# The seam between two graph layers of one fused kernel: moving the first queries and keys of layer 1 into the last turn of layer 0, and the last output products into sequence

## The chip, the core and the metric

The kernel runs on one core of a Trainium2 chip. The metric is device time in microseconds (us), the median of three runs. A core has five engines with a queue of instructions each: PE (TensorE, matrix products), DVE (VectorE), ACT (ScalarE), POOL (GpSimd) and SP (SyncE, which here issues every DMA). They run side by side and wait for each other through semaphores; within an engine, order is that of the program.

## The reference, cut to what matters

128 graphs of 64 nodes, 768 features. Layer 0 is a graph attention of 12 heads with a gate, layer 1 a masked attention of 6 heads; each ends in a layer norm over a residual.

```python
# layer 0
h    = einsum('bnd,ade->bane', x, W);  th = tanh(h)
attn = leaky(th @ w_src + swap(th @ w_dst))          # masked by adj, softmax
fo   = elu(attn @ h + b)
gate = sigmoid(x @ H_w.T + H_b)
x1   = layernorm(x + gate * fo + (1 - gate) * x)
# layer 1
q, k, v = x1 @ Wq + bq, x1 @ Wk + bk, x1 @ Wv + bv   # 6 heads of 128
p    = softmax(q @ k.T / sqrt(128) + mask(adj))
out  = layernorm(x1 + (p @ v) @ Wf + bf)
```

## The kernel before, in words

Everything is float32. The 8192 rows are 64 tiles of 128 rows (two graphs each), taken as 32 pairs. Every large product (768 x 768 weight) is done by a seven-product block scheme: class `Job` (line 150) multiplies 7 combinations of input blocks with 7 combinations of weight blocks, each a group of three accumulating matmuls into a PSUM bank, and `way_out` (line 182) adds the results into the output on ACT and DVE. `step` (line 208) issues one product on PE and then the way out of the product before it. The weight combinations are four subtractions per weight (`weight_sums`, line 129: T1 to T4; the loaded blocks are B11, B21, B22 and, until it is overwritten, T3), the input combinations four more (`block_sums`, line 135). A job's product number picks its weight block: 1 B11, 2 B21, 3 B22, 4 T4, 5 T1, 6 T2, 7 T3. In names of tiles a product's bank starts with y, z or x.

**Layer 0** (lines 236 to 626). Turn p of a loop makes h and gate of pair p and, half a turn behind, finishes pair q = p - 1: it normalises attention, makes x1, and computes the value rows v of layer 1 from it. The 21 products of a turn are in a hand-written order, `TURN` (line 52); a letter is the job (h, g, v; u is v of the turn before, whose last two products come then), a digit the product. The other steps are hung on positions of that order by `at(pos, ...)` (lines 584 to 614): for a tile t, `probs_by_nodes` transposes its probabilities (pTp), `attend` multiplies them with h (av), `features` divides (rden, fo), `elu1`, `gated`, `stats` and `normed` make x1, `by_features` transposes it (x1Tp). A pair's second tile goes first: 63 before 62 in pair 31. The tiles pTp, av and x1Tp share two PSUM banks with the tag "m". Each turn writes x1, its transpose x1T and v to DRAM. The loop runs over 34 turns: turn 32 has no new pair, so only u4, u3 and the seven v products remain for PE, and turn 33 has the last two v products.

**Layer 1** (lines 629 to 877). 16 groups of four tiles. Its storage is a new pool, `sb1`, opened when `sb0` of layer 0 is closed; then bf, the three bias columns (`load_cols`, line 116), wq, the group's four blocks of x1T (a), adj, wk and wf are loaded in that order, and the weight sums are on DVE (lines 653 to 659); wq takes the storage of w0, wk that of hw, wf that of wv. For each group and each of three feature blocks fc, `woven` (line 831) runs a query job and a key job in the order `WOVEN` (line 46), one step of the generators beside it per product: `attention` of the block before (scores sp, softmax, transposes sT, context cp), `finish` (norms of the group before), or `residuals` (line 770: the x1 rows, plus bf on POOL, and the input sums of the output job on DVE). After a group's features come the output products of the group before. At the end (line 865 on, g = 16) the last attention and residuals are drained first, then the 14 output products of the last two pairs are woven, and their four norms follow.

PE, DVE, ACT and POOL follow the order of these calls; so does SP for its DMAs, and a DMA that has to wait (for its data or for the storage it writes) holds those behind it.

Of the kernel before, what the change touches and what calls it, by code (L numbers as in the profile page):

```python
# [9 lines left out]
F32 = mybir.dt.float32  # L10
# [40 lines left out]

TURN = [
# [6 lines left out]
def kernel(  # L59
# [61 lines left out]
    def load_weight(src, tag, name):  # L121

        w = wpool.tile([P, 7, HK, HALF], F32, tag=tag, name=name)
        view = src.rearrange("(kh kc p) (nh f) -> kh nh p kc f", p=P, kc=HK, nh=2)
        for block, kh, nh in ((B11, 0, 0), (B21, 1, 0), (B22, 1, 1), (T3, 0, 1)):
            nc.sync.dma_start(out=w[:, block], in_=view[kh, nh])
        return w

    def weight_sums(eng, w):
        eng.tensor_tensor(w[:, T1], w[:, T3], w[:, B11], ALU.subtract)  # L130
        eng.tensor_tensor(w[:, T2], w[:, B22], w[:, T1], ALU.subtract)  # L131
        eng.tensor_tensor(w[:, T4], w[:, B21], w[:, T2], ALU.subtract)
        eng.tensor_tensor(w[:, T3], w[:, B22], w[:, T3], ALU.subtract)

    def block_sums(eng, pool, tag, a11, a12, a21, a22, name):

        shape = [P, HK, a11.shape[-1]]
        s1, s2, s3, s4 = (
            pool.tile(shape, F32, tag=f"{tag}{i}", name=f"{tag}{i}_{name}", bufs=1)
            for i in range(1, 5)  # L140
        )
        steps = [
            lambda: eng.tensor_tensor(s1, a21, a22, ALU.add),  # L143
            lambda: eng.tensor_tensor(s2, s1, a11, ALU.subtract),
            lambda: eng.tensor_tensor(s3, a11, a21, ALU.subtract),
            lambda: eng.tensor_tensor(s4, a12, s2, ALU.subtract),
        ]
        return {1: a11, 2: a12, 3: s4, 4: a22, 5: s1, 6: s2, 7: s3}, steps
# [64 lines left out]
    def layernorm(dst, z, eps, name):  # L213
        stats = small.tile([P, 2, 6], F32, tag="stats", name=f"st_{name}")
        for half in range(2):
            V.bn_stats(stats[:, half, :], z[:, half * HALF : (half + 1) * HALF])  # L216
# [19 lines left out]
    with ExitStack() as ph:  # L236
        sb = ph.enter_context(tc.tile_pool(name="sb0", bufs=2))

        def load_rows(src, n, name):
            t = sb.tile([P, n], F32, name=name, bufs=1)  # L240
            nc.sync.dma_start(out=t, in_=src.partition_broadcast(P))
            return t

        def load_xT(p):
            t = sb.tile([P, KC, PAIR * P], F32, tag="xT", name=f"xT_{p}")
            nc.sync.dma_start(out=t, in_=xT[p])
            return t
# [9 lines left out]
        def sums_of(eng, tag, t, name):  # L257
            return block_sums(
                eng, sb, tag, t[:, :HK, :P], t[:, HK:, :P], t[:, :HK, P:], t[:, HK:, P:], name
            )  # L260

        xTs = {0: load_xT(0)}
        w0_w = load_weight(w0, "wa", "w0")
        hw_w = load_weight(hwT, "wb", "hw")
        wsd = sb.tile([P, 2, D], F32, name="wsd", bufs=1)
        nc.sync.dma_start(out=wsd[:, 0, :], in_=wdst.partition_broadcast(P))
        nc.sync.dma_start(out=wsd[:, 1, :], in_=wsrc.partition_broadcast(P))
        hb_bc = load_rows(hb, D, "hb_bc")
        b01_bc = load_rows(b0, E0, "b01_bc")
        A = {}  # L270
        A[0], x_steps = sums_of(G, "sx", xTs[0], "x0")
        for s in x_steps:
            s()
        weight_sums(V, w0_w)
        weight_sums(G, hw_w)
        V.tensor_scalar(b01_bc, b01_bc, 1.0, None, ALU.add)
        wv_w = load_weight(wv, "wc", "wv")
        weight_sums(V, wv_w)
# [75 lines left out]
        def products(t):  # L354

            h = st[t]["h"]
            th = sb.tile([P, 2, D], F32, tag="th", name=f"th_{t}")
# [195 lines left out]
        def value_sums(q):  # L553
            B[q], v_sums[q] = sums_of(V, "sv", x1Ts[q], f"v{q}")

        def x_sums(p):
            A[p], steps = sums_of(G, "sx", xTs[p], f"x{p}")
            for s in steps:
                s()

        v_sums = {}
        jobs = {}
        for p in range(NP + 2):
# [5 lines left out]

            plan = {}  # L570

            def at(pos, ok, *acts):
                if ok:
                    plan.setdefault(pos, []).extend(acts)
# [40 lines left out]

            for pos, (job, i) in enumerate(TURN):
                ok = {"h": new, "g": new, "v": old, "u": 0 <= p - 2 < NP}[job]
                if ok:
                    step(jobs["u" if job == "u" else job], int(i))
# [6 lines left out]
        flush()  # L626


    with ExitStack() as ph:
        sb = ph.enter_context(tc.tile_pool(name="sb1", bufs=2))  # L630
        W2 = PAIR * P

        bf_bc = sb.tile([P, D], F32, name="bf_bc", bufs=1)
        nc.sync.dma_start(out=bf_bc, in_=bf.partition_broadcast(P))
        bq_c, bk_c, bv_c = load_cols(bq, "bq_c"), load_cols(bk, "bk_c"), load_cols(bv, "bv_c")

        def load_group(g):

            blocks = []
            for m in range(2):  # L640
                for kh in range(2):
                    t = sb.tile([P, HK, W2], F32, tag=f"a{m}{kh}", name=f"a{m}{kh}_{g}", bufs=1)
                    nc.sync.dma_start(out=t, in_=x1T_d[2 * g + m][:, kh * HK : (kh + 1) * HK, :])
                    blocks.append(t)
            ad = load_adj(sb, GT * g, GT, f"adjg_{g}")
            bias = sb.tile([P, GT, N], F32, tag="bias", name=f"bias_{g}", bufs=2)
            V.tensor_scalar(bias, ad, 1.0, NEG1 / SCALE, ALU.subtract, ALU.mult)
            ops, steps = block_sums(G, sb, "sq", *blocks, f"q{g}")
            for s in steps:
                s()  # L650
            return ops, bias

        wq_w = load_weight(wq, "wa", "wq")
        weight_sums(V, wq_w)
        loaded = load_group(0)
        wk_w = load_weight(wk, "wb", "wk")
        weight_sums(V, wk_w)
        wf_w = load_weight(wf, "wc", "wf")
        weight_sums(V, wf_w)

        def feature_job(name, ops, w, fc, dst, b):


            def at(m, n):
                return dst[:, n, m * W2 : (m + 1) * W2]

            def bias(n):
                return b[:, n * HK + fc : n * HK + fc + 1]

            return Job(  # L670
                name,
                W2,
                lambda i, kc: (w[:, OF_B[i], kc, fc * P : (fc + 1) * P], ops[i][:, kc, :]),
                lambda mn, bk_: S.activation(at(*mn), bk_, AF.Identity, bias=bias(mn[1])),  # L674
                lambda mn, bk_: V.tensor_tensor(at(*mn), bk_, at(*mn), ALU.add),  # L675
                lambda bk_: S.activation(at(1, 0), bk_, AF.Identity, bias=bias(0)),
            )

        ctxT = {}

        def attention(g, fc, qT, kT, bias):


            v = sb.tile([P, GT, 2, E1], F32, tag="v1", name=f"v1_{g}_{fc}")
            for a in range(2):
                c0 = (a * J1 + fc) * E1
                for i in range(GT):
                    nc.sync.dma_start(
                        out=v[a * N : (a + 1) * N, i, :, :],
                        in_=v_d[GT * g + i][:, c0 : c0 + E1].rearrange("(g m) e -> m g e", m=N),  # L690
                    )
            yield
            yield
            yield
            sp = bank("m", f"sp_{g}_{fc}")
            for i in range(GT):
                for a in range(2):
                    for gr in range(2):
                        at = slice(i * P + gr * N, i * P + (gr + 1) * N)
                        T.matmul(  # L700
                            sp[gr * N : (gr + 1) * N, (i * 2 + a) * N : (i * 2 + a + 1) * N],
                            qT[:, a, at],
                            kT[:, a, at],
                            start=True,
                            stop=True,
                        )
            yield
            sc = sb.tile([P, GT, 2, N], F32, tag="sc", name=f"sc_{g}_{fc}")
            V.tensor_tensor(
                sc,  # L710
                sp.rearrange("p (i a m) -> p i a m", i=GT, a=2),
                bias.unsqueeze(2).to_broadcast([P, GT, 2, N]),
                ALU.add,
            )
            sc3 = sc.rearrange("p i a m -> p (i a) m")
            mx = small.tile([P, 2 * GT], F32, tag="mx1", name=f"mx1_{g}_{fc}")
            V.tensor_reduce(mx, sc3, AX.X, ALU.max)
            yield
            V.tensor_tensor(sc3, sc3, mx.unsqueeze(2).to_broadcast([P, 2 * GT, N]), ALU.subtract)
            S.activation(sc, sc, AF.Exp, scale=SCALE)  # L720
            yield
            yield
            den = small.tile([P, 2 * GT], F32, tag="den1", name=f"den1_{g}_{fc}")
            V.tensor_reduce(den, sc3, AX.X, ALU.add)
# [195 lines left out]
```

## Time and profile before

| | us |
|---|---|
| median of 3 runs (3020.79 to 3021.99) | 3021.93 |
| the profiled execution, device time | 3022.04 |
| its span, first to last instruction | 3020.0 |
| PE busy | 2931.3 (97%) |
| DVE busy | 1830.8 (61%) |
| ACT busy | 1006.5 (33%) |
| POOL busy | 805.5 (27%) |
| mean granted clock of PE | 0.986 of full |

The page gives one profiled execution: busy times of each engine, the span in 40 slices (75.5 us each; a digit is the busy share in tenths, PEclk the granted clock in tenths), queues of DMA, waits and groups of instructions. A line of the timeline has start and length in us, engine, line of the code, operation, output<-inputs, shape and count; brackets hold the idle time ahead of it on its engine and who ended it. A matmul group of three in the code shows as x6. The window view has, for a stretch, its length, busy time and count of PE, PEld, DVE, ACT and POOL, then the clock, the DMA share and GB/s. Layer 0 runs to about 1515 us of the span, layer 1 from about 1519 us.

### The profile page before, as it was taken

What the parts mean: (1) busy time and instruction counts of PE and PEld (TensorE: products, weight loads), DVE (VectorE), ACT (ScalarE), POOL (GpSimd) and SP (SyncE); (2) the same over time, 40 slices, a digit from 0 to 9 for tenths busy, and PEclk for the clock granted to TensorE, in tenths of its full rate; (3) what the DMA queues carried; (4) which work ended last, traced back from release to release, by engine and by line L of the source; (5) the groups of instructions that cost most, each with busy time, mean ns of one, the idle gap of its engine ahead of it and who ended that gap; (6) DMA issues with size and microseconds to landing.
All of it is one profiled execution on the core that took longest, in us unless ns stands there. A gap on an engine that the chain in (4) does not pass through costs nothing. (4 is left out here: it accounts for less than half of the span.)

```text
span 3020.0 us, 45321 instructions
## 1 busy us (share of the span) xinstructions
PE 2931.3 (97%) x18048; PEld 2029.7 (67%) x18048; DVE 1830.8 (61%) x3017; ACT 1006.5 (33%) x1761; POOL 805.5 (27%) x650
## 2 busy tenths in 40 slices
PE   6999999999999999999869999999999999999997
PEld 3666666666666666666558777787777787777784
DVE  5888888888888888888633344434344434344434
ACT  2444344344444444444412222222222222222221
POOL 4324324324323333333212111211211211211211
PEclk8999999999999999999879999999999999999998
DMA  4333333333333333333242111222111222111211
GB/s 168 115 112 109 116 118 107 112 120 112 108 121 114 109 117 119 107 113 114 90 146 86 62 57 58 85 85 79 62 57 57 85 85 79 62 57 57 85 64 63
DMA packets 174929, 284.81 MB, mean 94 GB/s; under 512 B 46208, under 2 KB 112768, under 8 KB 174720
## 3 DMA queue, kind: packets, MB, share of 16 engines
q1 hardware_dynamic: 174720, 281.92, 28.7%
q8 instruction: 143, 2.34, 0.3%
q14 instruction: 66, 0.54, 0.1%
HBM read 167.81 MB, written 101.06 MB: 89 GB/s over the span
## 5 line engine op out<-in xcount | busy, mean ns | idle before, releaser
L487 POOL TENSOR_TENSOR x<-gate,x 128x768 f32<-128x768 f32 x64 | 116.5, 1821 | 330.9 <-ACT gate L538 330.9
L780 POOL TENSOR_TENSOR y<-y,bf_bc 128x768 f32<-128x768 f32 x64 | 114.3, 1816 | 301.7 <-DMA y<-x1d 301.7
L804 DVE TENSOR_TENSOR y<-y_o,y 128x384 f32<-128x384 f32 x128 | 69.8, 553 | 178.0 <-PE y_o L173 171.0
L222 POOL TENSOR_TENSOR rs_b<-ve_b,minus_half 128x1 f32<-128x1 f32 x64 | 35.1, 549 | 483.6 <-DVE ve_b L220 480.7
L675 DVE TENSOR_TENSOR kT<-z_k,kT 128x256 f32<-128x256 f32 x96 | 40.5, 422 | 203.6 <-ACT kT L674 108.9
L173 PE MATMUL y_q<-a,wq 128*128 128x256 f32 x576 | 141.7, 382 | 17.4 <-DMA a<-x1Td 17.4
L360 POOL TENSOR_TENSOR th<-th,wsd 128x768 f32<-128x768 f32 x64 | 116.0, 1812 | 157.5 <-DVE th L359 157.5
L143 POOL TENSOR_TENSOR sq_q<-a,a 128x768 f32<-128x768 f32 x16 | 29.5, 1844 | 466.6 <-PE y_o L173 311.0
L674 ACT ACTIVATE qT<-y_q,bq_c 128x256 f32<-128x256 f32 x144 | 67.3, 468 | 244.6 <-PE y_q L173 222.8
L173 PE MATMUL y_k<-a,wk 128*128 128x256 f32 x576 | 144.9, 388 | 1.8 <-DMA wk<-in_wk_dram 1.8
L173 PE MATMUL y_g<-hw,sx_x 128*128 128x384 f32 x384 | 136.0, 491 | 10.5 <-DVE gate L336 10.5
L173 PE MATMUL z_k<-sq_q,wk 128*128 128x256 f32 x576 | 141.5, 382 | 4.1 <-DVE qT L675 4.1
L173 PE MATMUL y_o<-wf,so_o 128*128 128x384 f32 x384 | 134.4, 494 | 8.8 <-DVE y L804 8.8
L173 PE MATMUL y_h<-w,xT 128*128 128x384 f32 x384 | 136.3, 492 | 6.8 <-DMA w<-in_w_dram 6.8
L173 PE MATMUL y_k<-sq_q,wk 128*128 128x256 f32 x576 | 141.5, 382 | 0.7 <-DVE wk L131 0.7
L173 PE MATMUL y_q<-sq_q,wq 128*128 128x256 f32 x576 | 140.0, 379 | 0.0
L173 PE MATMUL z_q<-sq_q,wq 128*128 128x256 f32 x576 | 140.0, 379 | 0.0
L222 POOL TENSOR_TENSOR rs_a<-ve_a,minus_half 128x1 f32<-128x1 f32 x64 | 35.2, 551 | 383.9 <-DVE ve_a L220 383.9
L173 PE MATMUL z_v<-wv,sv_v 128*128 128x384 f32 x384 | 137.5, 495 | 0.1
L173 PE MATMUL z_h<-w,sx_x 128*128 128x384 f32 x384 | 137.6, 495 | 0.0
L173 PE MATMUL y_h<-w,sx_x 128*128 128x384 f32 x384 | 135.5, 490 | 1.7 <-DVE w L131 1.7
L173 PE MATMUL y_v<-wv,x1T 128*128 128x384 f32 x384 | 136.5, 492 | 0.6 <-ACT v L349 0.6
(163 smaller groups left out, 6718.7 us busy)
## 6 DMA issues: line engine op xcount, KB each, us to landing
xT<-in_xT_dram SPq DMA_DIRECT2D x32, 768.0 KB, 7.0
x<-in_x_dram SPq DMA_DIRECT2D x64, 384.0 KB, 3.5
dd<-dstd SPq DMA_DIRECT2D x128, 192.0 KB, 3.4
x1d<-x SPq DMA_DIRECT2D x64, 384.0 KB, 2.5
x1Td<-x1T SPq DMA_DIRECT2D x32, 768.0 KB, 4.8
vd<-v SPq DMA_DIRECT2D x64, 384.0 KB, 2.9
a<-x1Td SPq DMA_DIRECT2D x64, 384.0 KB, 3.3
v<-vd SPq DMA_DIRECT2D x384, 64.0 KB, 2.3
```

Of the source, the lines that this page charges most:

```text
L143: lambda: eng.tensor_tensor(s1, a21, a22, ALU.add),
L173: T.matmul(to[:, : self.n], lhsT, rhs, start=kc == 0 and not more, stop=kc == HK - 1, skip_group_check=more,)
L222: G.tensor_tensor(rstd, ve, minus_half, ALU.pow)
L360: G.tensor_tensor(th[:, 1, :], th[:, 1, :], wsd[:, 1, :], ALU.mult)
L487: G.tensor_tensor(xp, st[t]["gate"], xp, ALU.mult)
L674: lambda mn, bk_: S.activation(at(*mn), bk_, AF.Identity, bias=bias(mn[1])),
L675: lambda mn, bk_: V.tensor_tensor(at(*mn), bk_, at(*mn), ALU.add),
L780: G.tensor_tensor(y[:, i, :], y[:, i, :], bf_bc, ALU.add)
L804: V.tensor_tensor(at(*mn), b, at(*mn), ALU.add)
```

## The change

Layer 1 no longer starts after layer 0. Four things are different.

1. *Storage.* Layer 0's tiles are split in two pools. Those that only the h and gate half uses (xT, its sums, th, wsd, hb) are in `sb0r` on the right side, which is closed in turn 31; a pool `early` takes its place for the query and key tiles, the x1T blocks and their sums. The rest of layer 1 is in a pool that takes the place of `sb0`. Both new pools wait tile by tile for what lay there.
2. *Loads and sums.* wq and wk are loaded block by block in turn 31, as soon as w0's and hw's blocks have had their last product. T1 and T2 of wq go to POOL, T3 and T4 to DVE, all four of wk to POOL; of the first group's input sums the first two are on POOL, the last two on DVE. The bias columns are loaded as the first thing in the kernel. wf and bf are loaded beside the third feature block.
3. *Order.* Turn 32 follows a list of its own, `LAST`, with the query and key products of feature block 0 (q, k) and the first of block 1 (Q, K); its other steps move to the positions of `LAST_AT`. There is no turn 33. `LAST_REST` ends block 1.
4. *The end.* The last group's residuals are chained behind its attention, two steps per product, inside the output products of the group before, with storage in the `early` pool. The last two pairs' output products run one pair after the other (`ENDS`); each pair's norms run as soon as it can, and for the last tile the first half of the statistics is taken early.

```diff
+LAST = [
+    "u4", "u3", "q1", "q2", "k1", "k2", "q6", "q5", "q7", "Q1", "q4", "Q2", "q3", "k6", "k5", "k7",
+    "Q6", "k4", "k3", "v1", "v2", "v6", "v5", "v7", "K1", "v4", "v3",
+]
+LAST_REST = [(1, 2), (0, 5), (1, 6), (0, 7), (1, 5), (1, 7), (0, 4), (0, 3), (1, 4), (1, 3)]
+LAST_AT = {3: 3, 4: 4, 5: 6, 6: 8, 7: 9, 8: 11, 9: 12, 11: 15, 12: 16, 15: 20, 16: 20, 19: 22}
+
+ENDS = [
+    (0, 1), (0, 2), (0, 6), (0, 5), (0, 7), (1, 1), (0, 4), (0, 3), (1, 6), (1, 5),
+    (1, 7), (1, 2), (1, 3), (1, 4),
+]
...
+        e, e2 = eng if isinstance(eng, tuple) else (eng, eng)
         steps = [
-            lambda: eng.tensor_tensor(s1, a21, a22, ALU.add),
-            lambda: eng.tensor_tensor(s2, s1, a11, ALU.subtract),
-            lambda: eng.tensor_tensor(s3, a11, a21, ALU.subtract),
-            lambda: eng.tensor_tensor(s4, a12, s2, ALU.subtract),
+            lambda: e.tensor_tensor(s1, a21, a22, ALU.add),
+            lambda: e.tensor_tensor(s2, s1, a11, ALU.subtract),
+            lambda: e2.tensor_tensor(s3, a11, a21, ALU.subtract),
+            lambda: e2.tensor_tensor(s4, a12, s2, ALU.subtract),
         ]
...
-        for half in range(2):
+        for half in range(2) if last_half is None else (1 - last_half, last_half):
+            if half == last_half:
+                yield
             V.bn_stats(stats[:, half, :], z[:, half * HALF : (half + 1) * HALF])
...
+    bias_c = {k: load_cols(src, f"b{k}_c") for k, src in (("q", bq), ("k", bk), ("v", bv))}
...
+        def queries_begin():
+            ph_r.close()
+            pools["early"] = ctx.enter_context(
+                tc.tile_pool(name="early", bufs=2, side="right", reuse_waits="tile")
+            )
+            row_sums[:] = load_group(0, (G, V), lambda: (query_tiles(0, 0), query_tiles(0, 1)))
+            jobs["q"], jobs["k"] = feature_jobs(0, 0)
+            jobs["Q"], jobs["K"] = feature_jobs(0, 1)
...
-        for p in range(NP + 2):
+        for p in range(NP + 1):
...
+            if p == NP - 1:
+
+                q_sums = weight_sums(G, w0_w)[:2] + weight_sums(V, w0_w)[2:]
+                k_sums = weight_sums(G, hw_w)
+                for pos, block in ((2, B11), (3, B21), (8, T3), (15, B22)):
+                    at(pos, True, do(load_block, wq, w0_w, block))
+                for pos, block in ((6, B11), (9, B21), (19, T3), (19, B22)):
+                    at(pos, True, do(load_block, wk, hw_w, block))
+                at(16, True, q_sums[0])
+                at(18, True, queries_begin, q_sums[1])
+                at(19, True, lambda: all_of(row_sums[:2]))
+            if p == NP:
+                flush()
+                for act in plan.pop(0):
+                    act()
+                for pos, act in zip((1, 2, 2, 3, 4, 5, 7, 9), row_sums[2:] + q_sums[2:] + k_sums):
+                    plan.setdefault(pos, []).append(act)
+            for pos, (job, i) in enumerate(TURN if new else LAST):
...
+                if last:
+                    attend = chain(attend, residuals(g, True))
+                woven(pair, *[attend] * (1 + last))
                 drain(attend)
                 attend = nothing
-                done = finish(g - 1)
...
+        p = 2 * NG - 2
+        pair = out_job(p), out_job(p + 1)
+        woven(pair, done, done, order=ENDS[:9])
+        drain(done)
+        done = finish(p)
+        woven(pair, done, done, order=ENDS[9:-1])
+        n0, n1 = norm(p + 1, 0), norm(p + 1, 1, last_half=0)
+        step(pair[1], ENDS[-1][1])
+        next(n0)
+        next(n1)
+        drain(done)
         flush()
-        drain(done)
+        next(n0, None)
+        next(n1)
+        next(n1, None)
```

## The prediction

> **What bounds the kernel now.** I read the page's 40 slices first, then the waits of TensorE, then the stages with a hole, then the timelines there.
>
> ```profile
> PE   6999999999999999999869999999999999999997
> ...
> PEclk8999999999999999999879999999999999999998
> ```
>
> TensorE is full, at full clock, in both layers. There are three holes: the start, slices 20 and 21 (the change of layers, near 1500 us), and the end. An edit that only moves work of other engines is worth something there and nowhere else.
>
> ```profile
> PE y_q L173 <- DMA a<-x1Td: 17.4, 1, 17.4
> ...
> PE x1Tp L436 <- ACT x L226: 10.9, 2, 6.9
> PE y_o L173 <- DVE y L804: 8.8, 1, 8.8
> ...
> PE z_k L173 <- DVE qT L675: 4.1, 1, 4.1
> PE pTp L436 <- DVE rden L473: 2.5, 1, 2.5
> PE av L457 <- ACT pT L437: 2.5, 1, 2.5
> PE y_k L173 <- DMA wk<-in_wk_dram: 1.8, 1, 1.8
> ```
>
> These are whom TensorE waited for (total, times, longest). All but y_o and pTp lie in the change of layers; y_o is the end. pTp, in the first turns, is kept for later: it shows that the transposes of a tile wait until DVE has read the attention of the tile before, because both use the two PSUM buffers "m".
>
> The wait is only part of a hole, as the timeline of TensorE shows (start, duration, idle before):
>
> ```profile
> 1554.53 2.93 PE L173 MATMUL z_k<-sq_q,wk 128*128 128x256 f32 x6 [4.14 <-DVE qT L675]
> 1557.26 2.77 PE L173 MATMUL y_k<-sq_q,wk 128*128 128x256 f32 x6
> 1559.82 1.71 PE L173 MATMUL y_q<-a,wq 128*128 128x256 f32 x6
> 1561.36 1.46 PE L173 MATMUL z_q<-sq_q,wq 128*128 128x256 f32 x6
> ```
>
> Start to start a product of 256 columns takes 1.30 us (1561.36 to 1562.65). After the 4.14 us idle, two take 2.73 and 2.56: the clock had halved, which costs another 2.7.
>
> Loss of the change of layers: from 1474.26 (first transposes of turn 32) to 1562.65 are 88.4 us. The work in it, at steady durations: 9 products of 384 columns x 1.935, 12 of 256 x 1.296, 4 groups of transposes x 0.66, 2 attentions x 0.95 = 37.5. So **50.9 us** are lost: 38.0 of waits, 12.9 of slow clock. Loss of the end: 8.85 idle at 2985, then 10 products in 22.2 us instead of 19.35, together **11.7**; and 12.55 from the last product's end (3007.45) to the end of the span. TensorE's work is unchanged (the same products), so new span = old span less losses removed plus losses added.
>
> **The change, part by part.** Times are on the old clock.
>
> *Turn 31 gains six weight-block loads, a sum and SP issues.* At about 0.77 us of issue each, beside a DMA that ran at 0.29 of its share in this turn, and in gaps of SP's queue (1456 to 1461): nothing, TensorE hides it. Two more weight blocks and four feature blocks are issued after the dd, hx and x1Td transfers, from 1470.1 on, and the next x1d, x1Td and vd writes queue behind them; nobody waits soon for those. At the 375 GB/s that this queue reached at 1524 to 1540: x1Td lands near 1475, wq B22 1476.5, the blocks 1477.5, 1478.5, 1479.6, 1480.6, wk 1482 and 1484. TensorE asks for the first block at 1478.8. The 17.4 us wait goes.
>
> *Turn 32 is filled.* Its work in the new order, from the transposes to the last V product, is 45.4 us and could end at 1519.7. What comes late next? POOL gets two weight sums of wq, two block sums, then four of wk; DVE gets sq3, sq4, T4 and T3 ahead of, and among, the steps of the last two tiles. These rows price it:
>
> ```profile
> 1541.89 1.36 DVE L130 TENSOR_TENSOR wk<-wk 128x1152 f32<-128x1152 f32 x1 [3.40 <-DMA wk<-in_wk_dram]
> 1543.28 2.85 DVE L131 TENSOR_TENSOR wk<-wk 128x1152 f32<-128x1152 f32 x1
> 1546.16 1.36 DVE L132 TENSOR_TENSOR wk<-wk 128x1152 f32<-128x1152 f32 x1
> ```
>
> ```profile
> 1540.17 1.80 POOL L145 TENSOR_TENSOR sq_q<-a,a 128x768 f32<-128x768 f32 x1
> 1541.93 2.98 POOL L146 TENSOR_TENSOR sq_q<-a,sq_q 128x768 f32<-128x768 f32 x1
> ```
>
> POOL's operation starts 0.04 after DVE's and takes 1.17 longer; DVE's next takes until 1546.13, which is 1.2 after POOL's end. Two-input sums in SBUF on DVE and POOL take turns; each waits for the other's whole instruction. On POOL a weight sum takes 2.61 (hw at 17.9 us).
>
> So by hand: POOL T2 1476.5 to 1479.1, sq1 1480.1 to 1481.9 (after DVE's masked step), sq2 1482.9 to 1484.7 (after DVE's sq3). DVE's sq4 waits for sq2; residual, sq4, residual, T4 then alternate to 1490.7; only then come DVE's divisions for tile 63, first half at 1491.4 (1489.7 if sq4 gets in ahead of the residual). The transposes of tile 62, third step of the new order, wait for exactly that (the pTp row above), and TensorE reaches them at 1482.4. **New wait 8.2 us** (7.3 to 9.0), and then a slow clock, 2.7. Without the taking of turns the divisions would be at 1487: 5 us. Next, q4 needs ScalarE to have read q7, which stands in ScalarE's queue behind the exponential of tile 62 and the norm of tile 63: TensorE is there at 1503.4, ScalarE at 1506: **2.6**. The norm of tile 62 waits for POOL's power behind wk's last two sums, but TensorE has q3 to k7 meanwhile. Sum 8.2 + 2.7 + 2.6 = 13.5. Behind the turn, adjg is loaded after the last V writes (3 us to land plus their 2), its bias (1.9) holds DVE ahead of the first softmax, and wf's sums wait for their load: with 10 products between, 1.0, bounds 0 and 3.
>
> Two rules of the Trainium skill are weighed. "TensorE: Matmul & The Clock Gate", Part 1, has the clock halve after an idle window of about 3.4 us and recover after about as much work: 1.7 us lost for a stop. The rows above show 5.3 us at half clock, 2.7 lost; the trace decides (by the rule the sum is 1 us lower). "GPSIMD Engine Reference", Engine selection, speaks against the change: elementwise work belongs on VectorE, GpSimd is about twice as slow with two inputs. The rows agree (2.61 against 1.36), but of six sums only T2 stands in front of the wait: by the rule the change would be 1.25 us better with T2 on DVE. I keep the trace's 13.5.
>
> *The end.* The last group's attention advances two steps per product and its residuals follow in the same sequence, so the sums are ready before the last 14 products. From the timeline of 2944 to 2954: scores to normalised rows take DVE and ScalarE 5.1 us; the new order leaves 3 products, 5.8. The new order of products leaves one or more between a result and its reuse (1.94 against 0.56 plus 0.1 to read it). So 11.7 goes. Tail: after the last product DVE adds (0.56, late by 0.5 as two statistics are in front), half a statistic 0.5, 0.4, power 0.7, shift 0.25, ScalarE 1.05 = 4.2, and 3.44 from ScalarE's last end to the span's end as before: 7.65 instead of 12.55, 4.9 saved. Bounds 12 to 16.6, **16.6** taken.
>
> *The start.* The three bias columns (768 pieces of 4 bytes each) now stand ahead of xT on SP. Their cost, by stages of the old place:
>
> ```profile
> 1521.00:1522.00 1.00, 0.00 (x0) 0.00 (x0) 0.00 (x0) 0.00 (x0) 0.00 (x0) 0.50 0.70 155
> 1522.00:1523.00 1.00, 0.00 (x0) 0.00 (x0) 0.00 (x0) 0.00 (x0) 0.00 (x0) 0.50 0.79 9
> 1523.00:1524.00 1.00, 0.00 (x0) 0.00 (x0) 0.00 (x0) 0.00 (x0) 0.00 (x0) 0.50 1.02 62
> ```
>
> The last two columns are DMA share and GB/s: 2.5 us of engines for bytes worth 0.6 at 375 GB/s, so 1.9 of columns. The first 30 us are one full DMA stream whose last weight (wv, landing 27.3) starts everything: **+1.9**, bounds 1.5 (SP's issue alone) and 3.5 (one column's 3.4 to landing).
>
> *Storage split, tile-wise reuse.* In layer 0 and from group 1 on each buffer keeps its number; the order on each queue is as before. Nothing; below nothing excluded, since TensorE is full there; above, see the last rival.
>
> Sum: 3020.0 - 50.9 + 13.5 + 1.0 - 16.6 + 1.9 = 2968.9 of span; 2.04 lie around it (3022.04 against 3020.0), so 2970.9; the median is 0.11 under the profiled execution. **2971 us.**
>
> **Rivals.**
> - *Little new wait:* DVE and POOL overlap better or the blocks land earlier, the clock holds; loss 5 instead of 14.5: 2961. For it, DVE's and POOL's order in the lock is a matter of 0.1 us. Chance 0.2.
> - *A long chain:* POOL's 22 us of sums and powers decide the turn: both tiles' norms late, the clock falls twice, softmax waits for adjg: loss 25: 2981. For it, POOL has one queue and rs_a stands behind wk's sums. Chance 0.2.
> - *The end does not close:* sums still late by half, 8 of 16.6 gained: 2979. Against: 5.1 of 5.8, so tight. Chance 0.07.
> - *Slower:* the split storage adds a wait to each of the 47 feature turns of layer 1. If a turn waited for one transfer (2.3 us, v), 47 x 2.3 = 108 on top: 2971 + 108 = 3079. It decides from 1.1 us per turn. Against: buffers and queue order are those of before, where no such wait shows. Chance 0.03.
>
> **Numbers.** Likeliest 0.5. The range takes in the first three rivals nearly whole: 2959 to 2983. A difference under 0.2% (6 us) cannot be told from none. Faster 0.96, same 0.01, slower 0.03.
>
> **What would show it.** Right: no wait for a or wq; a TensorE wait of 7 to 9 us of pTp for DVE near 1482, slow clock behind it; last V product done near 1533; no y_o wait at the end; 7 to 8 us of tail; start shifted by 2. Wrong: pTp without a wait (2961), several waits for POOL or ScalarE (2981), or waits inside layer 1.

## The result and the profile after

The changed kernel takes 2975.74 us (median of 4 runs, 2975.3 to 2977.21), the kernel before 3021.53 (4 runs on the same chip): ratio 0.985, 95% interval 0.983 to 0.987. The profiled execution takes 2976.17 us with a span of 2974.4; TensorE is busy for 2921.3 of it at a mean clock of 0.994. The forecast was 2971, its range 2959 to 2983.

The same two rows of the 40 slices as before:

```profile
PE   5999999999999999999989999999999999999999
...
PEclk8999999999999999999999999999999999999999
```

Counted from one, slices 20 and 21 stood at 8 and 6 before; now only slice 21 is short, at 8. The end is full, and the first slice has lost a tenth. Now the waits of TensorE (total, times, longest), the lines that answer to those of before:

```profile
PE pTp L715 <- DVE rden L752: 8.3, 2, 4.8
...
PE y_q L203 <- ACT qT L319: 2.8, 2, 1.5
PE z_v L203 <- DVE v L629: 1.6, 1, 1.6
...
PE y_v L203 <- DVE sv_v L174: 1.5, 1, 1.5
PE y_k L203 <- ACT kT L319: 1.4, 1, 1.4
PE x_q L203 <- DMA a<-x1Td: 0.7, 1, 0.7
```

The waits of 17.4, 10.9, 8.8 and 4.1 us are gone, y_o of the end among them. New is the wait for tile 63's divisions (rden) that the prediction looked for: 4.8 of the 8.3 us, the other 3.4 lie in the first turns (2.5 before). Small waits for ScalarE and VectorE stand around it. Where the 45.6 us of span went, old and new place by place:

| | predicted, us | traces, us |
|---|---|---|
| loss at the change of layers, gone | -50.9 | -50.9 |
| new loss inside turn 32 | +13.5 | +13.4 |
| turn 31 | 0 | +1.5 |
| behind the turn (wf's sums, next blocks) | +1.0 | +1.9 |
| start | +1.9 | +4.7 |
| end (11.7 + 4.9 predicted) | -16.6 | -17.1 |
| not assigned | | +0.9 |
| sum | -51.1 | -45.6 |

The new loss is the time of turn 32 less its work: from its first transposes (1480.68) to the end of its last V product (1539.47) are 58.8 us, its work is 45.4. The end: last product over at 2967.2, tail 7.2 instead of 12.55, no wait in the last 14 products.

### The profile page after: what moved, and what is told of

Its sections match the earlier page's. It is cut to its first block, busy times and chain, and to the rows that moved or that the text cites. A ratio compares the mean times of both kernels' runs of the same rounds, so it can differ in the third digit from the quotient of the medians.

```text
span 2974.4 us, 45312 instructions
## 1 busy us (share of the span) xinstructions
PE 2921.3 (98%) x18048; PEld 2021.3 (68%) x18048; DVE 1819.8 (61%) x3013; ACT 1006.3 (34%) x1761; POOL 821.0 (28%) x654
## 4 chain that ended last, share of the span: by engine, by line
PE 95%; DVE 2%; DMA 2%; SPq 1%; ACT 0%; issue 0%; POOL 0%; POOLq 0%; DVEq 0%; ACTq 0%
PE y_o L203 8%; PE y_k L203 8%; PE y_h L203 8%; PE y_v L203 8%; PE y_g L203 8%; PE y_q L203 8%; PE z_h L203 4%; PE z_v L203 4%; PE z_o L203 4%; PE z_k L203 4%; PE z_q L203 4%; PE z_g L203 4%; PE x_o L203 2%; PE x_k L203 2%; PE x_v L203 2%; PE x_g L203 2%
## 5 line engine op out<-in xcount | busy, mean ns | idle before, releaser
L203 PE MATMUL y_g<-hw_wk,sx_x 128*128 128x384 f32 x384 | 136.5, 492 | 11.1 <-DVE gate L615 11.1
L203 PE MATMUL y_h<-w_wq,xT 128*128 128x384 f32 x384 | 137.4, 495 | 8.9 <-DMA w_wq<-in_w_dram 8.9
L203 PE MATMUL y_k<-a,hw_wk 128*128 128x256 f32 x576 | 144.6, 387 | 0.0
L203 PE MATMUL y_q<-a,w_wq 128*128 128x256 f32 x576 | 140.2, 379 | 1.5 <-ACT qT L319 1.5
L203 PE MATMUL y_q<-sq_q,w_wq 128*128 128x256 f32 x576 | 140.3, 380 | 1.4 <-ACT qT L319 1.2
L203 PE MATMUL y_k<-sq_q,hw_wk 128*128 128x256 f32 x576 | 140.1, 379 | 1.4 <-ACT kT L319 1.4
L203 PE MATMUL z_q<-sq_q,w_wq 128*128 128x256 f32 x576 | 140.1, 379 | 0.0
L203 PE MATMUL z_k<-sq_q,hw_wk 128*128 128x256 f32 x576 | 140.0, 379 | 0.0
L203 PE MATMUL y_v<-wv,sv_v 128*128 128x384 f32 x384 | 136.6, 492 | 1.5 <-DVE sv_v L174 1.5
L203 PE MATMUL z_h<-w_wq,sx_x 128*128 128x384 f32 x384 | 137.5, 494 | 0.0
```

The lines of the kernel that those rows point to most:

```text
L203: T.matmul(to[:, : self.n], lhsT, rhs, start=kc == 0 and not more, stop=kc == HK - 1, skip_group_check=more,)
```

## The experiments

All times below are medians of 4 or 5 runs beside the kernel before on the same chip (its medians lie between 3021.5 and 3022.7); the changed kernel's own median is 2975.74, its runs 2975.3 to 2977.21. The 95% interval of each ratio is about 4.5 us to either side. By it only two of these kernels differ from the changed one (`norms_first` and `best2`). For the other differences of 2.8 to 6.3 us the ground is that the runs do not overlap with those of the changed kernel, and the rows of the traces; below 1 us nothing is concluded from times. A name in brackets is that of a run.

**Columns later** (`cols_late`). The loads of the three bias columns move from the top into turn 2.

```diff
-    bias_c = {k: load_cols(src, f"b{k}_c") for k, src in (("q", bq), ("k", bk), ("v", bv))}
+    bias_c = {}
...
+            if p == 2:
+                for k, src in (("q", bq), ("k", bk), ("v", bv)):
+                    bias_c[k] = load_cols(src, f"b{k}_c")
```

> The changed kernel with one difference: the three bias columns are loaded in turn 2 of layer 0 instead of ahead of everything else. Theory: the 4.7 us by which layer 0 runs late all come from these three loads (2.1 us until the first product, 0.5 more until wv's sums, and about 2 us because the longer stops of TensorE bring a slower clock after them), so the run takes 2971 us (4.7 less than 2975.7), the first product starts at 6.8 us and the first V product of turn 31 at 1460.7 instead of 1465.4. First rival: the columns cost only the 1.9 us of the prediction and the rest is the new storage or order of layer 0; then 2973.8, with the V product at 1463.5. Second rival: the loads are paid wherever they stand; then no change.

Measured: 2972.09 (2971.64 to 2973.08), ratio 0.9833 (0.9818 to 0.9848); 3.65 us less. The first product starts at 7.03 instead of 8.88, the first V product of turn 31 at 1462.72 instead of 1465.43 (before: 1460.71). So the columns are the cause of most of the start's 4.7, not of all. These are the windows of the changed kernel in which they run (last two columns: DMA share, GB/s):

```profile
2.00:3.00 1.00, 0.00 (x0) 0.00 (x0) 0.00 (x0) 0.01 (x1) 0.00 (x0) 1.00 0.51 4
3.00:4.00 1.00, 0.00 (x0) 0.00 (x0) 0.00 (x0) 0.00 (x0) 0.00 (x0) 1.00 1.15 73
4.00:5.00 1.00, 0.00 (x0) 0.00 (x0) 0.00 (x0) 0.00 (x0) 0.00 (x0) 1.00 0.75 276
```

In the first two of these us the DMA share is 0.51 and 1.15 while 4 and 73 GB/s are moved; the kernel before moved 307 and 384 GB/s there. Layer 0 has the same code in all kernels here but for the columns: nine traces with them first have that V product at 1465.1 to 1467.3 (mean 1465.8), three with them later at 1461.2 to 1462.8 (mean 1462.2). That is 3.6 us, as the medians say. The rest, 1.5 us above the one trace of before, lies within what these traces differ among themselves: two kernels with columns late and equal code in layer 0 are 1.6 apart.

**Divisions first** (`divide_first`). sq4 and T4 of wq stand behind tile 63's divisions on VectorE.

```diff
-                for pos, act in zip((1, 2, 2, 3, 4, 5, 7, 9), row_sums[2:] + q_sums[2:] + k_sums):
+                for pos, act in zip((1, 9, 5, 3, 4, 5, 7, 9), row_sums[2:] + q_sums[2:] + k_sums):
```

> The changed kernel with one difference: in turn 32 the last sum of the first group's inputs (sq4) and the weight sum T4 of wq are issued on VectorE after the divisions of tile 63, not ahead of them. Theory: the divisions stood behind these two sums, each of which took turns with a sum on GpSimd; the divisions then start at about 1490 instead of 1495.4, the 4.84 us wait of the transposes pTp falls below 1 us and with it the slow clock behind it (2.4 us), so the time is 2969 us (6 to 7 less). Rival (a long chain): GpSimd's sums and ScalarE's queue decide the turn; the wait comes back later in the turn at q4 or k7, and at most 2 us are gained: 2974 or more.

Measured: 2975.92 (2975.1 to 2976.21); nothing gained, the theory falls. The wait for the divisions has gone (the 2.9 that is left lies in layer 0's first turns), and this has come instead:

```profile
PE y_q L203 <- ACT qT L319: 8.5, 2, 7.7
...
PE pTp L715 <- DVE rden L752: 2.9, 1, 2.9
```

Product q4 waits 7.7 us for ScalarE to have read q7. ScalarE stands at the exponential of tile 62, which waits for tile 62's divisions, and those are behind the steps of tile 63 on VectorE, whose rows are here (start, duration; the same rows take 0.96 in other turns):

```profile
1493.60 2.24 DVE L771 SCALAR_TENSOR_TENSOR ex<-ex,fo 128x768 f32<-128x768 f32 x1
1495.87 3.27 DVE L776 SCALAR_TENSOR_TENSOR ex<-gate,ex 128x768 f32<-128x768 f32 x1
1499.25 3.19 DVE L778 TENSOR_TENSOR x<-ex,x 128x768 f32<-128x768 f32 x1
```

Beside them GpSimd has two residuals and two sums of wk:

```profile
1490.32 4.71 POOL L766 TENSOR_TENSOR x<-gate,x 128x768 f32<-128x768 f32 x2
1494.98 3.35 POOL L149 TENSOR_TENSOR hw_wk<-hw_wk 128x1152 f32<-128x1152 f32 x1
1498.41 3.22 POOL L150 TENSOR_TENSOR hw_wk<-hw_wk 128x1152 f32<-128x1152 f32 x1
```

These end at 1495.03, 1498.33 and 1501.63, and VectorE's three steps each end 0.81 us later: each step waits for one of them. The loss in the turn is 13.5 us, much as in the changed kernel (13.4): not one wait but the queue of VectorE and GpSimd together sets it.

**All sums on VectorE** (`all_dve`). The same steps at the same places, on the other engine.

```diff
-            row_sums[:] = load_group(0, (G, V), lambda: (query_tiles(0, 0), query_tiles(0, 1)))
+            row_sums[:] = load_group(0, V, lambda: (query_tiles(0, 0), query_tiles(0, 1)))
...
-                q_sums = weight_sums(G, w0_w)[:2] + weight_sums(V, w0_w)[2:]
-                k_sums = weight_sums(G, hw_w)
+                q_sums = weight_sums(V, w0_w)
+                k_sums = weight_sums(V, hw_w)
```

> The changed kernel with one difference: all weight sums of wq and wk and the first group's input sums in turns 31 and 32 are on VectorE; GpSimd keeps only the residuals and the powers. Theory (VectorE's two-input operations and GpSimd's take turns): VectorE's rows return to 0.94 us for sq and 1.36 us for a weight sum, elu's first step from 3.03 to 0.95; it takes over about 10 us of sums and saves about 11.6 us of turns, so the turn is shorter by what GpSimd's slowness cost in front of the divisions: the wait for the divisions falls from 4.84 to about 3 us, the 1.47 us stop in turn 31 goes; 2971 to 2974 us in all. Rival: GpSimd's sums ran beside VectorE for the greater part and the durations in the records are only waiting for data; then the 10 us of sums come on top of VectorE's queue, the norms of the last two tiles come late, and the time is 2980 us or more.

Measured: 2978.81 (2978.41 to 2979.5), 3.1 more, neither the theory's 2971 to 2974 nor the rival's 2980. The time is nearer to the rival, but the rows say what the theory said: elu's step 0.95 instead of 3.03, weight sums 1.35 to 1.36, and the stop in turn 31 is gone. The loss is one of place. T2 and the first input sums now hold VectorE while they wait for their data (1.95 and 0.83 us idle), ahead of the masked attention of tile 62 and the additions into v; u3 waits 7.0 us for such an addition, and the turn loses 18.0.

**T1 on VectorE alone** (`t1_dve`). Only the first weight sum of wq changes its engine.

```diff
-                q_sums = weight_sums(G, w0_w)[:2] + weight_sums(V, w0_w)[2:]
+                q_sums = weight_sums(V, w0_w)[:1] + weight_sums(G, w0_w)[1:2] + weight_sums(V, w0_w)[2:]
```

> The changed kernel with one difference: the first weight sum of wq in turn 31 is on VectorE and not on GpSimd. Theory: the stop of 1.5 us in turn 31 came from this sum on GpSimd (2.95 us) beside VectorE's second input sum of v (2.85 us where 0.56 is usual); on VectorE it takes 1.36 us, the stop goes, and the stop of 1.6 us at u3 in turn 32 goes with it as VectorE is ahead there. As far as turn 32 is set by VectorE's queue and the landing of the wq and x1T blocks the gain is passed on: 2973 to 2974.5 us. Rival: the stop is the input sums' own place in VectorE's queue; no change, with the 1.5 us still there.

Measured: 2975.63 (2973.78 to 2975.9). The stop of 1.5 us has gone from the trace, so its cause is shown; but u3's wait has grown from 1.6 to 2.8 and turn 32 loses 14.1. By the medians the stop was worth nothing (the theory had 2973 to 2974.5), by the traces at most 1 us.

**wk's sums held back** (`wk_held`). The idea of `divide_first` carried on: wk's four sums behind GpSimd's power for tile 63, T4 behind tile 62's divisions, Q6 ahead of k6. In this kernel k4 follows k7 directly and adds to the bank before k7's result is read, so a part of the first group's keys comes out wrong; the instructions and their number are unchanged.

```diff
-    "u4", "u3", "q1", "q2", "k1", "k2", "q6", "q5", "q7", "Q1", "q4", "Q2", "q3", "k6", "k5", "k7",
-    "Q6", "k4", "k3", "v1", "v2", "v6", "v5", "v7", "K1", "v4", "v3",
+    "u4", "u3", "q1", "q2", "k1", "k2", "q6", "q5", "q7", "Q1", "q4", "Q2", "q3", "Q6", "k6", "k5",
+    "k7", "k4", "k3", "v1", "v2", "v6", "v5", "v7", "K1", "v4", "v3",
...
-                for pos, act in zip((1, 2, 2, 3, 4, 5, 7, 9), row_sums[2:] + q_sums[2:] + k_sums):
+                for pos, act in zip((1, 9, 8, 3, 7, 7, 8, 8), row_sums[2:] + q_sums[2:] + k_sums):
```

> The changed kernel with three differences in turn 32: sq4 and T4 of wq behind the divisions of tiles 63 and 62 on VectorE; all four weight sums of wk on GpSimd behind its power for tile 63's norm; product Q6 ahead of k6 to give them time. Revised theory: what sets the turn is VectorE's queue from the divisions of tile 63 to those of tile 62, stretched because GpSimd's sums of wk take turns with elu, gate and residual (rows of 2.2, 3.3 and 3.2 us where 0.95 is usual, once the divisions come first); ScalarE's exponential of tile 62 and then product q4 wait for its end. With wk's sums held back these three rows return to about 1.0 us, the wait of q4 falls from 7.7 to about 2 us and its slow clock goes: 2968 to 2970 us against 2975.9. Rival: wk's sums then end too late and k6 or k5 waits instead for GpSimd or the norms of tile 62; 2974 us or more.

Measured: 2978.51 (2977.94 to 2980.69). Two of tile 63's three rows return to 0.96, q4's wait falls to 2.8; but tile 62's rows now take 3.03, 3.26 and 3.25 beside the sums, sq4 stands behind them, and q3 waits 5.5 us for it. The rival is right: the wait moves on.

**Another division of turn 32** (`turn_dve`). All sums on VectorE (as in `all_dve`), each where its data have landed, and only those in front of a division that products need soon. Not shown here: T2 and the first two input sums leave turn 31 for turn 32, and tile 62 is transposed two places later.

```diff
-    "u4", "u3", "q1", "q2", "k1", "k2", "q6", "q5", "q7", "Q1", "q4", "Q2", "q3", "k6", "k5", "k7",
-    "Q6", "k4", "k3", "v1", "v2", "v6", "v5", "v7", "K1", "v4", "v3",
+    "u4", "u3", "q1", "q2", "k1", "k2", "q6", "q5", "q7", "Q1", "q4", "Q2", "q3", "Q6", "k6", "k5",
+    "k7", "K1", "k4", "v1", "v2", "v6", "v5", "v7", "k3", "v4", "v3",
...
-                for pos, act in zip((1, 2, 2, 3, 4, 5, 7, 9), row_sums[2:] + q_sums[2:] + k_sums):
+                for pos, act in zip((0, 1, 1, 2, 3, 8, 8, 8, 8, 10, 10), q_sums[1:2] + row_sums[:3] + q_sums[3:] + q_sums[2:3] + row_sums[3:] + k_sums):
```

> The changed kernel with another division of the sums and another order of turn 32: all sums of wq, wk and the first inputs are on VectorE, at places where their data have landed; those that the divisions of tiles 63 and 62 do not need stand behind them (T4 of wq, sq4, T1 and T2 of wk behind the second, T3 and T4 of wk behind the gate of tile 62); Q6 stands ahead of k6, K1 ahead of k4, k3 behind v7, and tile 62 is transposed behind K1. Theory: VectorE and GpSimd share one resource for sums in storage, so that their added time sets turn 32 (about 45 us of such rows in 44 us); a weight sum costs it 1.36 us on VectorE and 2.6 us on GpSimd. With 6 weight sums and 2 input sums moved about 9 us of it are saved, and no sum stands in front of the divisions: the turn is shorter by 6 to 8 us, 2968 to 2970 us. Rival: the order of the steps (not their engine) or ScalarE's queue sets the turn, and as in the run with the same sums on VectorE at their old places nothing is gained: 2974 to 2979 us.

Measured: 2972.8 (2971.85 to 2973.59), 2.9 less, about half of what the theory gave; the turn loses 10.9. The three rows of tile 63 again, in this kernel:

```profile
1494.28 0.94 DVE L771 SCALAR_TENSOR_TENSOR ex<-ex,fo 128x768 f32<-128x768 f32 x1
1495.26 0.96 DVE L776 SCALAR_TENSOR_TENSOR ex<-gate,ex 128x768 f32<-128x768 f32 x1
1496.32 0.96 DVE L778 TENSOR_TENSOR x<-ex,x 128x768 f32<-128x768 f32 x1
```

2.9 us for what took 8.7 beside GpSimd in `divide_first`. q4's wait is 0.6. The order of steps alone gained nothing (`divide_first`, `wk_held`), the engine alone lost 3.1 us (`all_dve`); the gain needs both. What is left is k7, 3.8 us: ScalarE reads k6 behind the norm of tile 62.

**With columns late and wf early** (`best`). The kernel above with the columns in turn 2, wf's load ahead of block 1's last products.

```diff
+        f_sums = last_weight()
+        next(f_sums)
         for g in range(NG):
...
-            rows = residuals(g - 1, False) if g > 0 else last_weight()
+            rows = residuals(g - 1, False) if g > 0 else f_sums
```

> The kernel of the run beside it (sums of turn 32 on VectorE, its other order) with two more differences: the three bias columns are loaded in turn 2 of layer 0, and wf is loaded ahead of the last products of feature block 1 so that its sums do not wait. Theory: the gains add up: 3.7 us of the columns and 1.2 us of the wait for wf on top, so 4 to 5 us below the run beside it, 2963 to 2966 us. Rival: the moved load of wf delays the v rows or blocks of the next group that stand behind it on SyncE's queue; then no more than the 3.7 us of the columns.

Measured: 2969.42 (2967.21 to 2969.62), 3.4 less than `turn_dve`. That is the rival's number, the columns; the theory's 2963 to 2966 built on `turn_dve`'s own forecast of 2968 to 2970, and against its measured time asked for 4 to 5. The early load had nothing to take away: TensorE's 1.24 us of wait behind wf's sums (changed kernel) are already missing in `turn_dve`, where VectorE waits 0.56 us for wf and not 1.79. With the early load the scores wait 0.5 us for VectorE, and layer 1 is no shorter (1369.1 against 1368.7 us from the last V product to the first product of the last-but-one pair of outputs). The 3.4 us are also a balance: this trace reaches turn 32 6.1 us earlier than that of `turn_dve`, which is the latest of the nine above, and loses 3.0 us more in it.

**The two waits left** (`best2`). sq3 behind tile 63's divisions, tile 62's statistics ahead of T3 and T4 of wk, its norm on ScalarE behind the reading of k6.

```diff
-LAST_AT = {3: 3, 4: 4, 5: 6, 6: 8, 7: 9, 8: 11, 9: 12, 11: 17, 12: 18, 15: 20, 16: 20, 19: 22}
+LAST_AT = {3: 3, 4: 4, 5: 6, 6: 8, 7: 9, 8: 11, 9: 15, 11: 17, 12: 18, 15: 20, 16: 20, 19: 22}
...
-                for pos, act in zip((0, 1, 1, 2, 3, 8, 8, 8, 8, 10, 10),
+                for pos, act in zip((0, 1, 1, 3, 3, 8, 8, 8, 8, 11, 11),
```

> The kernel of the last run (sums of turn 32 on VectorE, columns late, wf early) with three steps of turn 32 moved: the third input sum sq3 stands behind the divisions of tile 63, the statistics of tile 62 ahead of the sums T3 and T4 of wk, and the norm of tile 62 on ScalarE behind its reading of k6. Theory: the two waits of TensorE that are left in the turn go, 2.7 us of pTp (sq2 and sq3, 2.5 and 2.1 us, stood in front of the divisions because they took turns with GpSimd's residuals) and 3.8 us of k7 (ScalarE's norm of tile 62 stood in front of its reading of k6), with about 3 us of slow clock behind them: 2961 to 2964 us. Rival: one of the waits is only moved on (to q7, to the transposes of tile 62 or to the first V product); 2966 us or more.

Measured: 2965.83 (2962.38 to 2966.77), ratio 0.9812 (0.9798 to 0.9825) to the kernel before: the fastest of all, 9.9 us below the changed kernel, whose interval (0.983 to 0.987) lies above this one. The turn loses 7.0. The median lies between the forecast (2961 to 2964) and the rival (2966 or more); small waits have come up elsewhere:

```profile
PE sp L347 <- DVE kT L320: 1.8, 1, 1.8
PE y_q L203 <- ACT qT L319: 1.3, 1, 1.3
PE y_k L203 <- DVE hw_wk L152: 1.3, 1, 1.3
```

**The end, in parts** (`residuals_after`). First: the last residuals not inside the products of the group before, but after its attention, as the kernel before had it.

```diff
-                if last:
-                    attend = chain(attend, residuals(g, True))
-                woven(pair, *[attend] * (1 + last))
+                woven(pair, attend)
                 drain(attend)
+                if last:
+                    drain(residuals(g, True))
```

> The changed kernel with one difference: the last group's attention advances one step per product as before the change, and its residuals and input sums are made after it, ahead of the last 14 products, not inside the products of the group before. The new order of the last products stays. Theory: the wait of TensorE for the first input sum returns (8.8 us before the change) and the slow clock after it (about 2.7 us): 2987 us (11.4 more). Rival: the new order of the last products is what removed most of the loss of the end, and the sums matter little: under 4 us more.

Measured: 2975.91 (2975.42 to 2976.76). Nothing is lost; the theory falls. The trace of before near the end shows why (SyncE, GpSimd, VectorE):

```profile
2973.18 4.91 SPq L826 DMA_DIRECT2D out_dram<-y  x4
2978.25 2.54 SPq L774 DMA_DIRECT2D y<-x1d  x2
```

```profile
2982.80 7.10 POOL L780 TENSOR_TENSOR y<-y,bf_bc 128x768 f32<-128x768 f32 x4 [6.48 <-DMA y<-x1d]
```

```profile
2976.48 0.55 DVE L143 TENSOR_TENSOR so_o<-ctxT 128x384 f32<-128x384 f32 x1
...
2984.63 0.56 DVE L804 TENSOR_TENSOR y<-y_o,y 128x384 f32<-128x384 f32 x1 [4.07 <-POOL y L780]
```

TensorE was ready at 2976.4 and waited until 2985.2 for a bank that VectorE had to add to the rows first. Two orders held that addition. On VectorE the eight input sums stood behind the four norms and were over at 2980.6. On SyncE's queue the loads of the rows stood behind four writes of results, which waited for the same norms; the rows came at 2982.8, and VectorE was idle for them for 4.1 us more. The change puts the sums ahead of the norms and the loads ahead of the writes, and so does the kernel just run; only the place inside the products of the group before is given up. In the next kernel (`norms_first`) the norms go in front again, which brings both orders back:

```diff
                 drain(attend)
-                if last:
-                    drain(residuals(g, True))
                 attend = nothing
                 done = finish(2 * g - 2, 2 * g - 1)
+                if last:
+                    flush()
+                    drain(done)
+                    drain(residuals(g, True))
```

> The changed kernel with the last group's residuals not only after its attention (as in the run before, which cost nothing) but also behind the four norms of the pair of output products before, as in the kernel before the change. The new order of the last products stays. Theory: the loss of the end came from SyncE's queue, in which the loads of the last residual rows stood behind the four writes of the results of the group before, and these waited for their norms; the rows then land late, GpSimd's four additions of bf follow (7 us), and VectorE's additions, the banks and TensorE wait for them. So a wait of about 9 us returns with a slow clock behind it: 2984 to 2988 us. Rival: the wait came from the order of the last products (two pairs side by side with three banks); with the new order no more than 3 us are lost.

Measured: 2990.17 (2988.8 to 2991.29), 14.3 more than without it and more than the theory's 2984 to 2988. SyncE's queue in this kernel, then TensorE and VectorE:

```profile
2944.00 4.91 SPq L476 DMA_DIRECT2D out_dram<-y  x4
2949.02 1.96 SPq L431 DMA_DIRECT2D y<-x1d  x4
```

```profile
2955.46 4.21 PE L203 MATMUL y_o<-wf,sq_o 128*128 128x384 f32 x6 [12.10 <-DVE y L462]
2959.46 2.99 PE L203 MATMUL z_o<-wf,sq_o 128*128 128x384 f32 x6
```

```profile
2954.84 0.56 DVE L462 TENSOR_TENSOR y<-y_o,y 128x384 f32<-128x384 f32 x1 [3.45 <-POOL y L438]
```

The wait is back, 12.1 us, with 2.9 of slow clock in two products, and that in the new order of products. The rival is out. But the theory is only a part: of the 12.1 us, 8.0 pass until the norms and the sums are through VectorE (2943.4 to 2951.4), then 3.5 until the rows are there, and 0.6 for the addition. What each of the two orders is worth alone was not run. Second part (`weave_ends`): the old order of the last 14 products and the four norms behind them.

```diff
-        woven(pair, done, done, order=ENDS[:9])
-        drain(done)
...
+        woven(pair, done, done)
+        drain(done)
+        flush()
+        drain(finish(p, p + 1))
```

> The changed kernel with the old order of the last 14 products (the two pairs side by side) and their four norms together after the last product; the residuals stay inside the products of the group before. Theory: only the tail is lost, 4.9 us by the prediction, 5.35 by the traces (12.55 against 7.2 us from the end of the last product): 2981 us, without a wait at the last products. Rival: the old order itself makes TensorE wait for banks that VectorE has to read, and the time is 2985 us or more.

Measured: 2981.23 (2980.25 to 2981.94), 5.5 more, without a wait in the products; the tail is 12.3 us again. As the theory said.

## Why the prediction was right, step by step

**Bound and gain.** Right: the change of layers lost 50.9 us before and loses nothing there now; TensorE's work is the same.

**Loads of turn 31 and 32.** No product of turn 32 waits for the blocks or weights. But "TensorE hides it" failed for T1, as GpSimd's and VectorE's rows show:

```profile
1469.35 2.95 POOL L149 TENSOR_TENSOR w_wq<-w_wq 128x1152 f32<-128x1152 f32 x1
```

```profile
1469.86 2.85 DVE L174 TENSOR_TENSOR sv_v<-sv_v,x1T 128x384 f32<-128x384 f32 x1
```

VectorE's second input sum of v took 2.85 us beside T1 and takes 0.56 without it (`all_dve`), and TensorE stopped for 1.5. The taking of turns that the prediction used for turn 32 was not applied to turn 31.

**The new wait.** The mechanism is right, its length was overstated and its neighbours were missed. VectorE's rows in the changed kernel:

```profile
1490.02 2.54 DVE L176 TENSOR_TENSOR sq_q<-a,sq_q 128x768 f32<-128x768 f32 x1 [1.63 <-POOL sq_q L174]
1492.49 2.95 DVE L151 TENSOR_TENSOR w_wq<-w_wq 128x1152 f32<-128x1152 f32 x1
1495.36 0.18 DVE L752 RECIPROCAL rden<-av 128x6 f32<-128x6 f32 x1
```

and TensorE's behind them, with the slow clock (a product of 256 columns takes 1.30 from start to start, here 2.56 and 1.75):

```profile
1496.28 1.57 PE L715 MATMUL pTp<-ident,prob 128*128 128x128 f32 x6 [4.84 <-DVE rden L752]
1497.64 2.77 PE L203 MATMUL y_k<-a,hw_wk 128*128 128x256 f32 x6
1500.20 1.91 PE L203 MATMUL x_k<-a,hw_wk 128*128 128x256 f32 x6
```

4.8 of wait against 8.2 predicted, 2.4 of slow clock against 2.7 (the clock rule's 1.7, an estimate from half speed for the page's 3.4 us, is further off), q4 1.5 against 2.6. The terms that are missing are u3 (1.6, the addition into v is behind a masked step that took 1.56 instead of 0.96 beside T2) and k7 (1.4, ScalarE's norm in front of its reading). By starts the delays are u4 0.45, u3 1.86, pTp 5.1, slow clock 2.4, q4 1.7, k7 1.6: 13.1 of 13.4.

Why did the sum still meet 13.5? Counted from the turn's first transposes, the wait ended after 15.6 us, where the prediction had 15.4 to 17.1; so the divisions came about when it said. TensorE came to them after 10.8 us and not 8.1, mostly because u4 and u3 had held it. What u3 lost was taken off the wait: VectorE's queue beside GpSimd sets the time up to that place, and the rival of the long chain came nearer to this than the forecast. Behind it, that k7's 1.6, which was missed, met what q4 and the clock fell short is luck. A wait taken away comes back as another one (`divide_first`, `wk_held`).

Of the two rules, the one of "GPSIMD Engine Reference", Engine selection, was priced too low: 1.25 us, for T2's slowness alone. sq1 and sq2 were on GpSimd in front of the wait as well, and the row above shows VectorE idle for sq2 for 1.63 us. With all sums on VectorE at fitting places the gain is 2.9 us, and with three more steps moved it is 6.5 (3.6 more from `best` to `best2`): a sum on GpSimd holds up VectorE too. The page "SBUF — State Buffer", section "SBUF: two separate sides", says just that: a VectorE operation with two inputs in SBUF and a GpSimd operation that reads SBUF shut each other out for a whole instruction. The rows of elu, 0.95 alone and 3.03 beside, agree.

**Behind the turn.** Predicted 1.0, measured 1.24 and 0.70. The first is the sum of wf, as supposed: it waits 1.79 us for its load, in front of the softmax on VectorE. The second is the next group's x1T blocks, which were not in the sum.

**The end.** Size right (16.6 against 17.1), and the tail (7.65 against 7.2; the steps listed for it add up to 3.96 and not 4.2, so that 7.4 was meant, and they took 3.97). Of the cause only half was seen. "The sums are ready before the last 14 products" is true, but it is enough that they stand ahead of the norms; that they lie inside the products of the group before is worth nothing (`residuals_after`). The other half, the loads of the rows behind the writes on SyncE's queue, has no term in the prediction, and that the change put it right as well is luck. The rival "end does not close" was argued about the attention's chain, which did not hold TensorE.

**The start.** The mis-sized term. The price of 1.9 was taken from the time that the DMA engines were busy for the columns at their old place; it comes out at 3.6, just above the bound of 3.5. In the traces the first product starts 2.1 us late, wv's sums 3.6 late (30.9 against 27.3), and the product that waits for them 2.6 late, after 11.15 us idle and not 10.5. The slow clock in the two products from there on makes it 4.1 (the next starts at 44.5 against 40.4).

**Storage and rivals.** TensorE has no wait in the trace after 1581.5, where layer 1 begins its second group, until the end, so the rival that was slower is out. The forecast missed by 4.7 us, of which start and turn 31 make 4.3 by the traces.

## What to carry to other kernels

Where two engines shut each other out of a resource, add their times up before placing a step, in every stage that the change touches: taking away one wait there only shows the next. Before a wait is put down to late arithmetic, look at what every queue holds in front of the operands, that of the transfers too: here norms in front of sums and writes in front of loads were worth 14 us together, and the weaving of the sums into earlier products nothing. Small transfers at the head of a saturated start can cost more than the time for which they keep the DMA engines busy (3.6 against 1.9 us here).

## What the runs showed of the hardware

- Three loads of 768 pieces of 4 bytes each cost 3.6 us in front of a full stream, and nothing that stands out in turn 2.
- The slow clock after a stop varied: 2.9 us lost after 4.1 idle (before, with the third product), 2.4 after 4.8 (changed), 1.8 after 2.8 and again after 5.5 (`wk_held`), 3.0 after 7.7 (`divide_first`). Idle time does not order it. "TensorE: Matmul & The Clock Gate", Part 1, has a window that runs freely, so that the same stop costs differently from run to run; that fits, and also that the first product took 4.17 and 3.73 us in two kernels with the same code there (`best`, `best2`).
- The same turn 32 lost 10.9 us in one kernel and 13.9 in another that reaches it 6 us earlier (`turn_dve` and `best`). What differs is when the residuals on GpSimd fall upon the input sums on VectorE: in `best` one gets in ahead of sq2, which takes 2.46 us and not 0.96. There sq1 had waited 0.53 us for its x1T block, and in `turn_dve` it had not; whether that is the reason stays open.
